# A Mamba block with linear attention and an fp8 FFN: the norms' reciprocal roots and the FFN's middle casts on ScalarE

## The chip, the core and the metric

The kernel runs on one core of a Trainium2 chip. A core has five engines with queues of their own, which run their instructions in the order of the queue: TensorE (PE, matrix products; its weight loads are listed as PEld), VectorE (DVE), ScalarE (ACT), GpSimd (POOL) and SyncE (SP), which here only issues DMAs. They share an on-chip memory (SBUF); products land in PSUM banks. The metric is the device time of one execution in microseconds (us).

## The reference

The input `x` is 8 images of 96 channels and 64 x 64 pixels; each image is a sequence of 4096 tokens. Layer 0 adds a Mamba block to `x`, layer 1 a linear attention and a two-layer FFN, each behind a norm. Cut to what is computed:

```
# layer 0:  x = x + mamba(groupnorm(x))
xz = u @ in_proj.T;  xm, z = halves of 192 channels
xm = silu(causal conv of 4 taps over xm)
dt, Bm, Cm = split(xm @ x_proj.T)                  # 6, 16, 16
delta = softplus(dt @ dt_proj.T + b)
h_t = exp(delta * A) * h_{t-1} + delta * Bm * xm   # 192 channels x 16 states
y = sum over states(h * Cm) + xm * D
out = layernorm((y * silu(z)) @ out_proj.T) * gamma + beta

# layer 1, on tokens t
t = t + (q @ (k.T @ v) * 16**-0.5, 6 heads) @ Wff + bff     # of layernorm(t)
h = relu(q16(q16(q8(layernorm(t)) @ q8(W1).T) + q8(b1)))
t = t + q16(q16(q8(h) @ q8(W2).T) + q8(b2))
```

`q8` rounds to a float of 5 exponent and 2 mantissa bits, `q16` to one of 5 and 10. A layernorm is (v - m) / sqrt(var + eps).

## The kernel before

The 8 images are 4 pairs (`p`), each sequence 8 chunks (`c`) of 512 tokens: 32 chunks in order. A chunk is 24 units (`u`, lines 711 to 765): three blocks of 64 channels (`j`), four groups of states (`g`), two halves of a group (`b`). A unit holds 128 partitions (4 states by 32 channels) by two images by 512 tokens. For unit u:

- GpSimd multiplies `dbu = du * b` three units ahead (`products_b`, L659).
- ScalarE makes `da = exp(A * delta)` into PSUM, one unit ahead, in two halves (`decay`, L681). There are two `da` buffers, so a half can start only when the scan that reads the same buffer a unit before is done.
- VectorE scans `hs = da * hs + dbu`, twice (L741), and multiplies by C from PSUM, `pr = hs * cc` (L763). In the units of `POOLED = (4, 5, 12, 13, 20, 21)` GpSimd makes this product instead, as `pooled`, at the start of the next unit (L770); those units have no product on VectorE.
- TensorE makes `cc` (`rows_c`, L671) and, for each pair of units, sums `pr` over states into the bank `y` (`sums`, L695, four matmuls). `gate` (L709) multiplies the sum by silu(z). For pooled pairs `sums` is called three units later, under `u - 3 in POOLED and u % 2 == 0`. For the last pair this would be u = 24, which does not come: its product is made, and not summed.
- ScalarE copies the last state of each unit (L719).

Everything else runs as generators, stepped by hand between the scans. `STEPS` names for each unit which chains take a step before the scans (left of the bar) and behind them (right of it); a star starts a chain. G is the group norm of the next pair; P prepares a chunk two ahead (convolution, silu, softplus, delta); E does a chunk's output projection, layernorm, residual and Gram matrix; W makes attention weights; F0 and F1 do attention and FFN for the two images of a chunk 9 earlier (`LAG`). So F0 and F1 run from chunk 9 on. The order inside the loop is the order of the program (`tc.manual_schedule()`). After the last scan the remaining chains are interleaved by `run_out`, and there, as in the prologue, the framework's scheduler orders the instructions.

An F chain (`chain_f`) goes: load tokens; attention product on TensorE (L962); residual add on VectorE (L968); layernorm of four tiles (`norm_stats` on VectorE, four GpSimd instructions, `normalise` on ScalarE, L420); transposes; cast to fp8; three hidden products (L989), each rounded to f16 (L997) and passed through bias and relu on ScalarE (L1007; on VectorE in the tail, L1003) and cast to fp8 on GpSimd (L1011); the product with W2 (L1033); rounding and bias `y16` (L1038, L1042); transposes of the residual (L1045); and the final add `res` on VectorE (L1048).

GpSimd's small work is put off: `later(kind, work)` puts it on a list, `now(kind)` issues what is there, `settle(job)` issues it early if a reader comes first. `now("norms")` stands at the start of a unit, `now("others")` behind its scans. A norm's GpSimd work is a multiplication by -1 (L412), an addition of eps (L131), a power of -1/2 (L132) and a product (L414); 128 norms run, two per E chain (8 tiles) and one per F chain (4 tiles). Silu, softplus and exp use different tables on ScalarE, so loads stand between them.

Of the kernel before, what the change touches and what calls it, by code (L numbers as in the profile page):

```python
# [39 lines left out]
    2: "| E* F0 F1 G6 F1",  # L40
    3: "F1 F0 P | F1 G6",
    4: "| E",
    5: "| W0* P F1 E",
# [22 lines left out]
def tile_mamba_linear_attention_ffn(  # L66
# [59 lines left out]
    mhalf = const.tile([128, 8], F32, name="mhalf")  # L126
    nc.vector.memset(mhalf, -0.5)

    def rsqrt(out_, var, eps):

        nc.gpsimd.tensor_scalar_add(out_, var, eps)  # L131
        nc.gpsimd.tensor_tensor(  # L132
            out_, out_, mhalf[0 : out_.shape[0], 0 : out_.shape[1]], op=ALU.pow
        )
# [264 lines left out]
    def norm_stats(src, n, tag):  # L399

        mv = p2.tile([128, n, 2], F32, tag=f"mv{tag}", name="mv")
        rstd = p2.tile([128, n], F32, tag=f"rs{tag}", name="rs")
        nmr = p2.tile([128, n], F32, tag=f"nm{tag}", name="nm")
        st = p1.tile([128, n, 6], F32, tag=f"st{tag}", name="st")
        for i in range(n):
            nc.vector.bn_stats(st[:, i, :], src[:, i, :])  # L406
        for i in range(n):
            nc.vector.bn_aggr(mv[:, i, :], st[:, i, :])


        def ends():
            nc.gpsimd.tensor_scalar_mul(nmr, mv[:, :, 0], -1.0)  # L412
            rsqrt(rstd, mv[:, :, 1], 1e-5)
            nc.gpsimd.tensor_mul(nmr, nmr, rstd)  # L414

        return rstd, nmr, later("norms", ends)

    def normalise(dst, src, norm, q):
        settle(norm[2])
        nc.scalar.activation(  # L420
            dst, src, AF.Identity, bias=norm[1][:, q : q + 1], scale=norm[0][:, q : q + 1]
        )
# [4 lines left out]
    def load_x(p, c):  # L427
# [8 lines left out]
        )  # L436
        x_next[p, c] = t

    def chain_p(p, c, s, after):
# [52 lines left out]
        nc.scalar.activation(xm, xm, AF.Silu)  # L492
        nc.scalar.activation(zs, zs, AF.Silu)
        yield
        dbl = p1.tile([C, T], F32, tag="dbl", name="dbl")
# [18 lines left out]
        for j in range(NJ):  # L514
# [5 lines left out]
            nc.scalar.activation(delta[:, j, :], ps, AF.Identity, bias=dtb[:, j : j + 1])  # L520
        nc.scalar.activation(delta, delta, AF.Softplus)
        yield
        for part in ((0,), (1, 2)):
# [17 lines left out]
    def first_p(s, after):  # L541
# [51 lines left out]
        for j in range(NJ):  # L593
# [11 lines left out]
            if not j:  # L605
                for to in ("du", "dl"):
                    s[to, 0] = p2.tile([128, 4, T], F32, tag=to, name=to)
                for b in range(2):
                    for n in range(NG):
                        for to, of, queue in (("du", "lu", nc.sync), ("dl", "ld", nc.scalar)):  # L610
# [5 lines left out]
                            )  # L616

        cs = s["cs"] = p2.tile([128, T], F32R, tag="cs", name="cs")
        nc.vector.tensor_copy(cs[64:96], ps[64:96, :])
# [91 lines left out]
    def unit(s, prev, nxt, first, u, steps):  # L711
# [16 lines left out]
        if u - 3 in POOLED and u % 2 == 0:  # L728
            sums(s, u - 3)
        if u % 2 == 0 and (u or prev is not None) and (u - 1) not in POOLED:  # L730
            sums(s if u else prev, (u or NU) - 1)
# [3 lines left out]
        if to is not None:  # L735
            products_b(to, v)
        hs = s["hs", u] = p2.tile([128, 2, T], F32, tag="hs", name="hs", bufs=3)
        dbu = s.pop(("dbu", u))
# [199 lines left out]
    def chain_f(p, c, b, banks, lane=None):  # L938
# [45 lines left out]
        h16 = []  # L984
        casts = []

# [12 lines left out]
        def relu(m):  # L999
# [6 lines left out]
            else:  # L1006
                nc.scalar.activation(h16[m], h16[m], AF.Relu, bias=b1q[:, m : m + 1])  # L1007
            casts.append(
                later(
                    "others",  # L1010
                    lambda: nc.gpsimd.tensor_copy(h8[0][:, m, :], h16[m], saturate=False),  # L1011
                )
            )

# [13 lines left out]
        yield  # L1028
        for job in casts:
            settle(job)  # L1030
        ps = psum(bank)
# [78 lines left out]

    waiting.update(norms=[], others=[])
    with tc.manual_schedule():
# [26 lines left out]
    for kind in list(waiting):  # L1139
        now(kind)  # L1140
        del waiting[kind]
    s = slots[N - 1]
    sums(s, NU - 1)
    gate(s, NJ - 1)
# [82 lines left out]
```

## Time and profile before

The median of three runs is 3163.89 us (3163.77 to 3164.42). The profiled execution spans 3160.5 us from its first to its last instruction; the rest of its time, some 3.4 us against that median, lies around the span.

| stretch, us | length | PE busy | DVE busy | ACT busy | POOL busy |
|---|---|---|---|---|---|
| prologue, 0 to 70 | 70 | 41.9 | 26.2 | 20.6 | 13.2 |
| 70 to 1000 | 930 | 733.0 | 908.0 | 630.2 | 861.1 |
| 1000 to 2000 | 1000 | 787.9 | 957.4 | 760.6 | 934.9 |
| 2000 to 3008 (last scan) | 1008 | 792.6 | 966.5 | 761.4 | 947.6 |
| tail, 3008 to 3160.5 | 152.5 | 114.3 | 77.0 | 91.0 | 83.9 |

| group | count | busy, us | mean, ns |
|---|---|---|---|
| POOL dbu, L659 | 768 | 1804.6 | 2371 |
| DVE scan, L741 (with a state pointer) | 1290 | 1573.5 | 1265 |
| ACT decay, L681 | 1474 | 1000.6 | 688 |
| POOL power, L132 | 128 | 173.3 | 1354 |
| POOL cast, L1011 | 192 | 117.6 | 622 |
| ACT table loads (L681, L492, L521) | 125 | 160.4 | 1283 |

How to read it: a line of the waits says which engine and line waited, on which engine and line, for how long in total, how often, and the longest. A line of the timeline gives start, length, engine, line, operation, output and input tiles, shape and count, and in brackets the idle time before it with what ended it. A merged line (x2, x4) covers several instructions. The first scan of chunk 15 starts at 1419.1 us; a unit with a product on VectorE takes 3.69 us, one without 2.4.

### The profile page before, as it was taken

Reading aid. Unit: us, or ns where it says so; the run is one execution under the profiler, and the core shown is the slowest. Engines: PE = TensorE matmul, PEld = TensorE weight load, DVE = VectorE, ACT = ScalarE, POOL = GpSimd, SP = SyncE. Lnnn points to the kernel's source line nnn. Section 1 sums busy time; section 2 is a strip of 40 time slices with the busy share of each in tenths; the row PEclk is TensorE's granted clock in tenths of the full one; section 3 lists DMA queues with packets and bytes.
Section 4 is the critical chain, followed back from the end, with each engine's and each line's share of the span. In section 5 each row is a group of like instructions: output and inputs, shape, how many; then the busy total and the mean of one; then the engine's idle time right before and its main releaser. Section 6 shows DMA issues by size and latency. Waiting matters only on the chain. (4 is left out here: it accounts for less than half of the span.)

```text
span 3160.5 us, 35127 instructions
## 1 busy us (share of the span) xinstructions
PE 2469.6 (78%) x9450; PEld 928.7 (29%) x9450; DVE 2935.2 (93%) x4265; ACT 2263.9 (72%) x4360; POOL 2840.7 (90%) x1921
## 2 busy tenths in 40 slices
PE   6787787878787777777777778777888778887777
PEld 2122222222222223222233323222323222332344
DVE  4999999999999999999999999999999999999945
ACT  3666666667677777777777777777877777777656
POOL 2999999999999999999999999999999999999955
PEclk8677777787778888888888877898888888877668
DMA  6655556665555667555667555567565466755322
GB/s 149 152 122 137 134 156 152 160 150 135 141 143 135 138 162 175 146 129 125 141 164 170 141 146 125 137 157 170 146 148 127 124 144 162 169 132 134 95 70 73
DMA packets 253037, 443.75 MB, mean 140 GB/s; under 512 B 37605, under 2 KB 45990, under 8 KB 252838
## 3 DMA queue, kind: packets, MB, share of 16 engines
q1 hardware_dynamic: 247846, 439.40, 56.9%
q10 hardware_dynamic: 4992, 2.11, 0.3%
q8 instruction: 74, 1.21, 0.2%
q14 instruction: 125, 1.02, 0.1%
HBM read 349.11 MB, written 92.27 MB: 140 GB/s over the span
## 5 line engine op out<-in xcount | busy, mean ns | idle before, releaser
L659 POOL TENSOR_TENSOR dbu<-du,b 128x1024 f32<-128x1024 f32 x768 | 1804.6, 2371 | 112.6 <-DVE hs L741 65.5
L741 DVE TENSOR_TENSOR_SCAN hs<-da,state,dbu 128x512 f32<-128x512 f32 x1290 | 1573.5, 1265 | 25.6 <-ACT da L681 24.6
L681 ACT ACTIVATE da<-dl,aneg 128x512 f32<-128x512 f32 x1474 | 1000.6, 688 | 665.4 <-DVE hs L741 644.2
L763 DVE TENSOR_TENSOR pr<-hs,cc 128x1024 f32<-128x1024 f32 x576 | 698.7, 1213 | 35.1 <-DVE hs L741 0.5
L695 PE MATMUL y<-pr,ssum 128*32 128x512 f32 x2816 | 585.1, 831 | 113.3 <-DVE pr L763 113.3
L770 POOL TENSOR_TENSOR pr<-hs,c 128x1024 f32<-128x1024 f32 x192 | 453.8, 2363 | 36.6 <-DVE hs L741 30.4
L459 PE MATMUL mp<-u,wk 96*64 96x512 f32 x1488 | 398.1, 658 | 66.6 <-ACT xm L477 66.4
L671 PE MATMUL cc<-cs,sel 64*128 64x512 f32 x576 | 330.0, 583 | 144.8 <-DVE pr L763 144.4
L671 PEld LDWEIGHTS cc<-cs,sel 64*128 64x128 f32 x576 | 121.6, 215 | 557.3 <-DVE pr L763 296.8
L741 DVE TENSOR_TENSOR_SCAN hs<-da,dbu 128x512 f32<-128x512 f32 x184 | 213.2, 1205 | 17.4 <-POOL dbu L659 9.9
L516 PE MATMUL mp<-dbl,dtT 12*128 12x512 f32 x186 | 158.9, 947 | 56.8 <-ACT cs L506 38.5
L695 PEld LDWEIGHTS y<-pr,ssum 128*32 128x32 f32 x2816 | 87.9, 132 | 380.6 <-DVE pr L763 201.6
L791 PE MATMUL mE<-woT,zs 128*128 128x192 f32 x744 | 146.6, 350 | 66.7 <-ACT t1e L799 45.1
L459 PEld LDWEIGHTS mp<-u,wk 96*64 96x64 f32 x1488 | 97.0, 145 | 293.6 <-issue 156.6
L132 POOL TENSOR_TENSOR rs<-rs,mhalf 128x8 f32<-128x8 f32 (+1 forms) x128 | 173.3, 1354 | 10.7
L791 PEld LDWEIGHTS mE<-woT,zs 128*128 128x128 f32 x744 | 127.3, 200 | 126.8 <-ACT t1e L799 70.5
L703 PE MATMUL y<-xm,dd 128*128 128x512 f32 x192 | 129.2, 760 | 22.4 <-DVE zs L709 21.9
L467 PE MATMUL mp<-u,wz 96*64 96x512 f32 x372 | 137.0, 825 | 4.3 <-ACT xm L485 4.3
L1011 POOL CAST h<-h 128x512 fp8e5<-128x512 f16 x192 | 117.6, 622 | 24.8 <-DVE h L1003 15.8
L719 ACT COPY state<-hs 128x2 f32<-128x2 f32 x736 | 130.1, 181 | 0.2
L420 ACT ACTIVATE o<-x,nm,rs 128x96 f32<-128x96 f32 x256 | 98.6, 455 | 36.4 <-POOL nm L414 34.4
L531 POOL TENSOR_TENSOR du<-delta,xm 128x512 f32<-128x512 f32 x93 | 117.1, 1273 | 0.0
(306 smaller groups left out, 3234.1 us busy)
## 6 DMA issues: line engine op xcount, KB each, us to landing
du<-lu SPq DMA_DIRECT2D x380, 256.0 KB, 5.5
dl<-ld SPq DMA_DIRECT2D x380, 256.0 KB, 7.9
b<-bd SPq DMA_DIRECT2D x512, 128.0 KB, 5.0
lu<-du SPq DMA_DIRECT2D x96, 256.0 KB, 5.7
ld<-delta SPq DMA_DIRECT2D x93, 256.0 KB, 2.4
c<-bd SPq DMA_DIRECT2D x128, 128.0 KB, 4.4
xg<-in_x_dram SPq DMA_DIRECT2D x32, 384.0 KB, 3.8
xr<-in_x_dram SPq DMA_DIRECT2D x32, 384.0 KB, 8.7
```

The costliest lines, as they stand in the source:

```text
L132: nc.gpsimd.tensor_tensor(out_, out_, mhalf[0 : out_.shape[0], 0 : out_.shape[1]], op=ALU.pow)
L459: nc.tensor.matmul(ps[64 * b : 64 * b + 64, :], lhsT=wk[:, k, 64 * j : 64 * j + 64], rhs=u[:, b, k : k + T], start=(k == 0), stop=(k == 3),)
L467: nc.tensor.matmul(ps[64 * b : 64 * b + 64, :], lhsT=wz[:, 64 * j : 64 * j + 64], rhs=u[:, b, 3 : T + 3], start=True, stop=True,)
L516: nc.tensor.matmul(ps, lhsT=dtT[:, j, :], rhs=dbl[0 : 2 * RANK, :], start=True, stop=True)
L659: nc.gpsimd.tensor_mul(dbu, s["du", j][:, 2 * b : 2 * b + 2, :], s["b", g][:, b, :].unsqueeze(1).to_broadcast([128, 2, T]),)
L671: nc.tensor.matmul(cc, lhsT=sel[64:128, g, b], rhs=s["cs"][64:128, :], start=True, stop=True)
L681: nc.scalar.activation(da, s["dl", j][:, 2 * b + h, :], AF.Exp, scale=aneg[:, 2 * j + h, g : g + 1])
L695: nc.tensor.matmul(s["y"][q : q + 32, :], lhsT=ssum, rhs=pr[:, h, :], start=False, stop=(g == NG - 1),)
L741: nc.vector.tensor_tensor_scan(hs[:, h, :], s.pop(("da", u, h)), dbu[:, h, :], 0.0 if first else state["last"][:, u, h : h + 1], ALU.mult, ...
L763: nc.vector.tensor_mul(pr, hs, s.pop(("cc", u)).unsqueeze(1).to_broadcast([128, 2, T]))
L770: nc.gpsimd.tensor_mul(pr, s["hs", u], s["c", g][:, b, :].unsqueeze(1).to_broadcast([128, 2, T]))
L791: nc.tensor.matmul(ps[:, 2 * k * C : 2 * (k + 1) * C], lhsT=zs[:, j, tok : tok + 128], rhs=woT[:, j].rearrange("p b c -> p (b c)"), start= ...
```

## The change

Four edits. (1) A norm's root is computed on ScalarE, as exp(-0.5 * ln(var + eps)), and ScalarE makes its negative; one product by the mean stays on GpSimd, on a new list `shifts`, issued behind `products_b`. A call `exp_and_ln` loads the table set that holds both functions behind each silu, each softplus and the prologue. (2) The casts of the FFN's middle layer go to ScalarE, directly behind the relu, in the loop; in the tail they stay on GpSimd. (3) The pair of units 20 and 21 is summed, at u = 0 of the next chunk and behind the last. (4) F0's fourth step (the normalise) moves from the front of unit 3 to the back of unit 4.

```diff
-    3: "F1 F0 P | F1 G6",
-    4: "| E",
+    3: "F1 P | F1 G6",
+    4: "| F0 E",
...
+    eps5 = const.tile([128, 1], F32, name="eps5")
+    nc.vector.memset(eps5, 1e-5)
...
-        def ends():
-            nc.gpsimd.tensor_scalar_mul(nmr, mv[:, :, 0], -1.0)
-            rsqrt(rstd, mv[:, :, 1], 1e-5)
-            nc.gpsimd.tensor_mul(nmr, nmr, rstd)
-
-        return rstd, nmr, later("norms", ends)
+        def power():
+            nc.scalar.activation(rstd, mv[:, :, 1], AF.Ln, bias=eps5)
+            nc.scalar.activation(rstd, rstd, AF.Exp, scale=-0.5)
+            nc.scalar.mul(nmr, rstd, -1.0)
+
+        def shift():
+            nc.gpsimd.tensor_mul(nmr, nmr, mv[:, :, 0])
+
+        return rstd, nmr, (later("norms", power), later("shifts", shift))
...
+    def exp_and_ln():
+        nc.scalar.preload_act_table_set("natural_log_exp_and_others")
...
         nc.scalar.activation(xm, xm, AF.Silu)
         nc.scalar.activation(zs, zs, AF.Silu)
+        exp_and_ln()
...
         nc.scalar.activation(delta, delta, AF.Softplus)
+        exp_and_ln()
...
+        if u == 0 and prev is not None:
+            sums(prev, NU - 3)
...
         now("norms")
         steps(u, 0)
         to, v = at(u + AHEAD)
         if to is not None:
             products_b(to, v)
+        now("shifts")
...
-            casts.append(
-                later(
-                    "others",
-                    lambda: nc.gpsimd.tensor_copy(h8[0][:, m, :], h16[m], saturate=False),
-                )
-            )
+            if after:
+                nc.gpsimd.tensor_copy(h8[0][:, m, :], h16[m], saturate=False)
+            else:
+                nc.scalar.activation(h8[0][:, m, :], h16[m], AF.Copy, saturate=False)
...
-        for job in casts:
-            settle(job)
...
+    sums(s, NU - 3)
     sums(s, NU - 1)
```

## The prediction

> **What bounds the kernel now.** First the page, for the busy shares.
>
> ```profile
> span 3160.5 us, 35127 instructions
> PE 2469.6 (78%) x9450; PEld 928.7 (29%) x9450; DVE 2935.2 (93%) x4265; ACT 2263.9 (72%) x4360; POOL 2840.7 (90%) x1921
> ```
>
> VectorE and GpSimd are both near full, so the waits must say which of them the other serves. I asked for VectorE's waits between 70 and 3008 us (first to last scan), then for ScalarE's and TensorE's.
>
> ```profile
> DVE hs L741 <- ACT da L681: 31.7, 43, 1.2
> DVE res L1048 <- ACT da L681: 19.8, 18, 1.7
> DVE hs L741 <- POOL dbu L659: 9.9, 1, 9.9
> DVE x L968 <- PE mE L962: 6.4, 12, 0.9
> ```
> ```profile
> ACT y L1038 <- PE mF L1033: 46.2, 23, 3.0
> ACT o L420 <- POOL nm L414: 22.4, 22, 1.1
> ```
> ```profile
> PE mF L1033 <- POOL h L1011: 40.8, 61, 1.2
> ```
>
> A scan waited for GpSimd's product once in 1536 scans, at the start. In chunks 9 to 30 VectorE is idle about 3.7 us of some 94 per chunk, and 1.4 of that are gaps of 0.1 us between a scan and the product that needs it. So VectorE's own list is the bound; freeing GpSimd pays only through the chain cast, TensorE, ScalarE, VectorE that these lines trace. The timeline of chunk 15 shows that chain in units 15 and 16 (GpSimd, TensorE, ScalarE, VectorE):
>
> ```profile
> 1478.85 0.61 POOL L1011 CAST h<-h 128x512 fp8e5<-128x512 f16 x1
> 1479.42 0.93 POOL L818 TENSOR_TENSOR t1e<-t1e,gamma 128x384 f32<-128x384 f32 x1
> 1480.29 0.61 POOL L1011 CAST h<-h 128x512 fp8e5<-128x512 f16 x1
> ```
> ```profile
> 1480.95 0.58 PE L1033 MATMUL mF<-h,w2T 128*96 128x512 fp8e5 x1 [0.85 <-POOL h L1011]
> 1481.47 2.07 PE L516 MATMUL mp<-dbl,dtT 12*128 12x512 f32 x2
> 1483.47 1.09 PE L1045 MATMUL mF<-ident,x 128*96 128x128 f32 x4
> ```
> ```profile
> 1476.32 0.73 ACT L1007 ACTIVATE h<-h,b1q 128x512 f16<-128x512 f16 x1
> 1481.58 0.58 ACT L1038 CAST y<-mF 96x512 f16<-96x512 f32 x1 [2.25 <-PE mF L1033]
> ```
> ```profile
> 1485.01 0.69 DVE L1048 TENSOR_TENSOR res<-mF,y 96x512 f32<-96x512 f32 x1 [1.04 <-ACT delta L520]
> ```
>
> The last relu ends at 1477.05, its cast at 1480.90: it stood behind GpSimd's other work. TensorE is stuck in its queue until then, then runs L516 and L1045 back to back, and VectorE stands 1.04 us. The profile names ACT for that wait, but TensorE's L1045 ends 0.45 us before `res`; I read it as the releaser.
>
> **The change, part by part.** VectorE's and SyncE's orders in the built programs are the same until the tail, apart from one memset: every microsecond won or lost in the loop is VectorE idle time. The two-chain work (F0, F1) runs from chunk 9; units 4 to 16 have it in 22 chunks (10 to 31).
>
> *Casts leave GpSimd (gain).* 138 casts of 0.615 us (85 us of GpSimd time, hidden: no one in the loop waits for GpSimd but this chain). With the cast right behind the relu, L1033 can end about 2 us sooner in unit 15, L1045 ends about 1.3 us sooner, and `res` needs 1.04. So the idle before `res` goes: 19.8 + 2.1 + 1.3 (three rows of that wait) = 23.2 us. L962, next in the same unbroken TensorE run, goes with it: 6.4. Gain 29.6 us, bounds 0 and 29.6; I take all, since the margin is 1 us. Late next would be the third delta product.
>
> *Casts land on ScalarE (loss).* No row shows the cast there. Issue to issue, the relu on the same tile takes 0.62 us (1470.19 to 1470.81), the rounding copy out of PSUM 0.48; the cast is a plain copy like the second, of the first's tile and behind it: I take 0.55. In units 2, 15 and 23 it falls where ScalarE has slack (the decay waits for the scan; over 1.3 us in unit 15). Unit 13 has none:
>
> ```profile
> 1470.81 1.29 ACT L681 ACTIVATE da<-dl,aneg 128x512 f32<-128x512 f32 x2
> 1474.43 1.30 ACT L681 ACTIVATE da<-dl,aneg 128x512 f32<-128x512 f32 x2
> ```
> ```profile
> 1471.59 2.46 DVE L741 TENSOR_TENSOR_SCAN hs<-da,state,dbu 128x512 f32<-128x512 f32 x2 [0.67 <-ACT da L681]
> 1475.54 2.45 DVE L741 TENSOR_TENSOR_SCAN hs<-da,state,dbu 128x512 f32<-128x512 f32 x2
> ```
>
> Two casts are added there, one ahead of each of these decays. The first delays the scan at 1471.59 by its whole 0.55. The second: the decay ends at 1475.12 and its scan starts at 1475.54, 0.32 beyond the usual 0.10, so 1.10 - 0.55 - 0.32 = 0.23 more. 0.78 x 22 = 17.2 us; with 0.48 it is 0.64 x 22 = 14, with 0.62 it is 0.92 x 22 = 20.
>
> *F0's normalise moves from unit 3 to unit 4 (loss).* In unit 3 it waited 1.01 us for GpSimd's root. In unit 4, which has no product on VectorE (cadence 2.4 us, not 3.7), it stands ahead of the copy L799:
>
> ```profile
> 1438.69 0.47 ACT L799 COPY t1e<-mE 128x384 f32<-128x384 f32 x1
> 1439.06 0.19 ACT L719 COPY state<-hs 128x2 f32<-128x2 f32 x1
> 1439.23 0.69 ACT L681 ACTIVATE da<-dl,aneg 128x512 f32<-128x512 f32 x1
> ```
>
> Four normalises take 1.45 from start to next start (1432.92 to 1434.37). L799 then starts at 1440.14, the decay at 1440.60, ending 1441.29; its scan began at 1440.87. Loss 0.47 x 22 = 10.3 us. Bounds: 0 (if ScalarE is early by then) and 0.6.
>
> *Norms.* GpSimd loses three instructions of 0.25, 0.24 and 1.35 us per norm, 128 norms, 236 us, hidden as above. ScalarE gets three small ones, not shown before: between the state copy (2 elements, 0.181) and a normalise (96 elements, two pointers, 0.453); I take 0.25, as 4 or 8 elements are near the copy, so 0.75 per norm. They fall in units 3, 7, 17 and 18. Unit 3 loses the 1.45 and the 1.01 of waiting and gains 1.10 (two casts) + 0.75; unit 7 has ScalarE waiting for the scan (the decay has 1.6 us of slack); in 17 the slack is 2.3 or more; in 18 the decay is then late by about 0.55 of 1.69. Cost 0; at 0.453 each (1.36) still 0. The one multiplication left on GpSimd waits for ScalarE, but stands behind dbu, and the next dbu needs a scan that ends later.
>
> *Table loads.* 128 in both built programs, of 1.283 us. They move ahead of two state copies that never waited there: 0.
>
> *Sums.* TensorE gets 4 matmuls (8 records, 1.66 us) per chunk in unit 0, where it then idles 1.5 us for ScalarE's xm: 0. If that cover is gone, `gate` in unit 1 still has over 2 us.
>
> *Start and tail.* In the prologue the two small group matmuls (25.69 and 27.21 us) now stand behind two more pairs of transposes: +2 (0 to 3), on the path to the first scan. After the last scan (152 us, ScalarE busy 91, GpSimd 84) some 20 norms become about 0.7 us shorter (1.95 on GpSimd from first start to last end, against 0.75 + 0.2 + 0.3 of handing over) but cost ScalarE 0.75 each: bounds -14 and +15, I take -1.
>
> Sum: -29.6 + 17.2 + 10.3 + 2 - 1 = -1.1 us. The profiled execution spans 3160.5, 3.4 under the median of 3163.9, so 3162.8, or 3163.
>
> A rule against the change: under "Rules for kernel authors", the Trainium skill's page "ScalarE: Activation LUTs" would have simple elementwise work on VectorE rather than ScalarE. VectorE's nearest row (the f16 relu of the tail, 0.353 us) would put 138 x 0.353 = 49 us onto the engine that bounds this kernel, and the sum would be 3163 - 17 + 49 = 3195; the row decides for ScalarE here. The same page prices a plain ACTIVATE at 186 ns plus 0.833 per element, which makes the cast 0.61 us long by estimate, 0.52 issue to issue with its overlap of 0.09; the sum by it is some 1 us lower.
>
> **Rivals.**
> - *The idle before `res` stays* (slower). ScalarE reaches unit 15 already 1.1 us late, adds a third cast, and has decays and a delta copy ahead of y16. For: ScalarE has no slack from unit 10 to 14. Against: it now stands 2.25 us there. It decides if y16's copy starts less than about 1 us sooner. Price 23: 3186.
> - *The tail gets slower.* Its queues are interlocked, and ScalarE is busy 13.3 of 15 us near 3140. Up to +15: 3178.
> - *The losses are hidden* (faster). If the casts or the moved normalise find ScalarE early, 17 + 10 do not arise, or only half: 3136 to 3150. Against: the 0.10 us between decay and scan in nearly every chunk's unit 13 and 14.
> - *The tail gains* the whole 14: 3150.
> - *GpSimd's relief speeds VectorE itself.* Scans in the trace with GpSimd busy all along take 1.260 us in the median, with it idle 1.255: worth nothing.
>
> **How the numbers follow.** Offset within 0.2% (6.3 us, about what a measurement of this kernel can tell from no change): 0.38. `res` idle stays, or the cast is dearer than 0.62: 0.21; slow tail: 0.11; losses hidden: 0.20; tail gain: 0.10. So faster 0.30, same 0.38, slower 0.32. The range of the likeliest is 3157 to 3170. For 8 in 10 it reaches to half the hidden losses and the tail's gain together (3140) and past the first rival (3190).
>
> **What would show it.** Right: no idle before L1048 in unit 16 and no wait of L1033 for GpSimd in the loop; new waits of scans for decays in units 6, 14 and 15 of 0.5, 1.0 and 0.2 us; GpSimd at about 80%, ScalarE at 77%; no more than 128 table loads. Wrong: if units 7, 17 or 18 show waits for decays, the small norms cost more than I think; if the loop keeps its length and the end does not, it was the tail.

## The result and the profile after

The changed kernel takes 3205.8 us in the median (3202.9 to 3209.3), the kernel before 3163.9 on the same chip: a ratio of 1.0134, with a 95% interval of 1.0119 to 1.0148. The prediction said 3163, in a range of 3140 to 3190. The change costs 42 us, and the time is outside the range.

The page of the changed kernel, the busy shares:

```profile
span 3205.4 us, 35922 instructions
PE 2544.6 (79%) x9706; PEld 975.9 (30%) x9706; DVE 2948.8 (92%) x4266; ACT 2414.3 (75%) x4882; POOL 2533.9 (79%) x1399
```

GpSimd fell from 90% to 79% and ScalarE rose from 72% to 75% (forecast: about 80% and 77%). VectorE, whose list of work was to stay the same, is 13.6 us busier than before. Its waits, from first scan to last (which engine waited, for whom, us in total, times, longest):

```profile
DVE hs L756 <- ACT da L693: 59.3, 81, 1.7
DVE st L408 <- ACT t1e L814: 29.1, 27, 1.3
DVE hs L756 <- POOL dbu L671: 11.3, 2, 10.0
DVE res L1058 <- ACT da L693: 9.3, 9, 1.2
DVE x L983 <- PE mE L977: 6.1, 19, 0.4
```
```profile
POOL nm L419 <- ACT nm L416: 138.7, 51, 5.2
```

Scans wait 28 us more for their decays, much as predicted. The idle before `res` only halved (19.8 to 9.3). The second line is new and was not foreseen: the norm's statistics wait for the copy of `t1e`. GpSimd's wait before the one multiplication it kept, 139 us, does no harm to VectorE, as predicted: scans wait for GpSimd hardly more than before (11.3 us against 9.9).

The two traces can be laid side by side unit by unit, since VectorE does the same work in each unit: the time from a unit's first scan to the next unit's first scan, after minus before, summed over the chunks (us; units 5, 6, 13, 14, 16 and 17 over chunks 10 to 31, where F0 and F1 both run):

| place | predicted | measured |
|---|---|---|
| start, up to the first scan | +2 | +1.9 |
| units 16 and 17 (`res`, L968) | -29.6 | -12.6 |
| units 13 and 14 (two casts on ScalarE) | +17.2 | +22.2 |
| unit 5 (decay of unit 6 late) | +10.3 | +10.9 |
| unit 6 (statistics wait for `t1e`) | 0 | +26.7 |
| units 3 and 7 (small VectorE operations get long), all chunks | 0 | +9.9 |
| all other places of the loop | 0 | +3.4 |
| tail, after the last scan | -1 | -17.4 |
| sum | -1.1 | +45.0 |

The profiled executions differ by 44.9 us. Of the 3.4 us of other places, 4.0 arise at unit 6 in chunks 1 to 9 (the rest sums to a little under zero): there the copy is not late, and TensorE's same group of matmuls ran at another clock than before. Three lines carry the error: unit 6, the small operations, and the half of the `res` idle that stayed. A fourth, the tail, is an error to the other side. The experiments take these up.

**Unit 6 in the trace.** Chunk 15, ScalarE of the changed kernel, then TensorE and VectorE (start, duration, instruction, and the idle before it with its releaser):

```profile
1461.58 0.69 ACT L693 ACTIVATE da<-dl,aneg 128x512 f32<-128x512 f32 x1 [0.49 <-DVE hs L756]
1462.21 1.53 ACT L426 ACTIVATE o<-x,nm,rs 128x96 f32<-128x96 f32 x4
1463.64 0.46 ACT L814 COPY t1e<-mE 128x384 f32<-128x384 f32 x1
1464.00 0.19 ACT L731 COPY state<-hs 128x2 f32<-128x2 f32 x1
1464.10 1.30 ACT L693 ACTIVATE da<-dl,aneg 128x512 f32<-128x512 f32 x2
```
```profile
1464.15 4.21 PE L806 MATMUL mE<-woT,zs 128*128 128x192 f32 x12 [3.34 <-ACT t1e L814]
```
```profile
1467.26 0.39 DVE L408 BATCH_NORM_STATS2 st<-t1e 128x6 f32<-128x96 f32 x2
1468.91 1.06 DVE L408 BATCH_NORM_STATS2 st<-t1e 128x6 f32<-128x96 f32 x6 [1.26 <-ACT t1e L814]
```

F0's four normalises stand ahead of the copy L814. The prediction followed the copy's other neighbour on ScalarE, the decay of unit 6, and got its 0.5 us right. It did not ask who waits for the copy itself. The copy frees bank mE (a bank is one of the pieces of PSUM that products land in); TensorE waits for it with the second half of the projection (L806). In the kernel before the same group reads:

```profile
1439.21 2.22 PE L791 MATMUL mE<-woT,zs 128*128 128x192 f32 x12 [1.35 <-ACT t1e L799]
```

So TensorE's idle grew from 1.35 to 3.34 us, and the group itself from 2.22 to 4.21 us. The granted clock, from the table of stretches (stretch, its length, busy us and instructions of PE, PEld, DVE, ACT, POOL, then the clock), shows what goes with the longer group; the first line is of the kernel before, the second of the changed one:

```profile
1439.20:1441.40 2.20, 2.19 (x13) 1.96 (x13) 2.20 (x3) 1.72 (x4) 2.20 (x2) 1.00 0.00 0
```
```profile
1464.20:1468.30 4.10, 4.10 (x13) 3.66 (x13) 3.04 (x5) 1.80 (x3) 4.10 (x2) 0.50 0.66 160
```

The same matmuls ran at full clock before and at half after. Counted from the first scan of unit 5, the copy came 1.4 us later than before and the group ended 3.4 us later; the second copy of `t1e`, which used to be ready early, held up the statistics by 1.26 us.

**The small operations in the trace.** Group norm chain G, chunk 14, unit 7, VectorE and GpSimd of the changed kernel:

```profile
1374.94 0.16 DVE L178 TENSOR_TENSOR gndev<-gnm,gnmean 96x2 f32<-96x2 f32 x1
1375.13 2.21 DVE L179 TENSOR_TENSOR gndev<-gndev 96x2 f32<-96x2 f32 x1
1377.38 0.16 DVE L180 TENSOR_TENSOR gndev<-gndev,gnmv 96x2 f32<-96x2 f32 x1
```
```profile
1374.98 2.34 POOL L671 TENSOR_TENSOR dbu<-du,b 128x1024 f32<-128x1024 f32 x1 [0.68 <-DVE gnmean L177]
```

A square of two elements takes 2.21 us, and ends within 0.02 us of the end of GpSimd's product. Before, the same operations took 0.16 us each, beside GpSimd's power operation of the norm, which the change has taken away:

```profile
1355.33 0.16 DVE L177 TENSOR_TENSOR gndev<-gndev 96x2 f32<-96x2 f32 x1
1355.52 0.16 DVE L178 TENSOR_TENSOR gndev<-gndev,gnmv 96x2 f32<-96x2 f32 x1
```
```profile
1354.59 1.67 POOL L132 TENSOR_TENSOR rs<-rs,mhalf 128x8 f32<-128x8 f32 x1
```

### The profile page after: what moved, and what is told of

Its sections match the earlier page's. It is cut to its first block, busy times and chain, and to the rows that moved or that the text cites. A ratio compares the mean times of both kernels' runs of the same rounds, so it can differ in the third digit from the quotient of the medians.

```text
span 3205.4 us, 35922 instructions
## 1 busy us (share of the span) xinstructions
PE 2544.6 (79%) x9706; PEld 975.9 (30%) x9706; DVE 2948.8 (92%) x4266; ACT 2414.3 (75%) x4882; POOL 2533.9 (79%) x1399
## 3 DMA queue, kind: packets, MB, share of 16 engines
q8 instruction: 77, 1.26, 0.2%
## 4 chain that ended last, share of the span: by engine, by line
DVE 46%; PE 21%; ACT 18%; issue 11%; POOL 2%; DVEq 0%; DMA 0%; POOLq 0%; ACTq 0%
DVE hs L756 35%; DVE pr L778 6%; ACT da L693 4%; PE y L707 4%; PE mE L806 3%; PE mp L526 3%; DVE st L408 2%; PE cc L683 2%; ACT o L426 1%; PE mp L508 1%; ACT L446 1%; PE mp L468 1%; PE mE L822 1%; PE mF L1043 1%; DVE mv L410 1%
## 5 line engine op out<-in xcount | busy, mean ns | idle before, releaser
L707 PE MATMUL y<-pr,ssum 128*32 128x512 f32 x3072 | 620.0, 804 | 114.9 <-DVE pr L778 112.6
L468 PE MATMUL mp<-u,wk 96*64 96x512 f32 x1488 | 388.7, 623 | 46.3 <-ACT xm L486 44.2
L806 PE MATMUL mE<-woT,zs 128*128 128x192 f32 x744 | 188.7, 420 | 119.5 <-ACT t1e L814 94.3
L707 PEld LDWEIGHTS y<-pr,ssum 128*32 128x32 f32 x3072 | 96.8, 129 | 405.9 <-DVE pr L778 212.8
L806 PEld LDWEIGHTS mE<-woT,zs 128*128 128x128 f32 x744 | 165.5, 249 | 176.7 <-ACT t1e L814 124.0
L526 PE MATMUL mp<-dbl,dtT 12*128 12x512 f32 x186 | 166.3, 988 | 64.4 <-ACT cs L516 49.8
L419 POOL TENSOR_TENSOR nm<-nm,mv 128x8 f32<-128x8 f32 (+1 forms) x128 | 27.4, 214 | 163.4 <-ACT nm L416 152.3
L476 PE MATMUL mp<-u,wz 96*64 96x512 f32 x372 | 145.7, 872 | 4.2 <-ACT xm L494 4.2
L508 PE MATMUL mp<-xm,xpT 128*96 128x512 f32 x186 | 114.3, 763 | 2.9 <-DVE hs L756 2.9
```

What stands on the lines that cost most here:

```text
L468: nc.tensor.matmul(ps[64 * b : 64 * b + 64, :], lhsT=wk[:, k, 64 * j : 64 * j + 64], rhs=u[:, b, k : k + T], start=(k == 0), stop=(k == 3),)
L476: nc.tensor.matmul(ps[64 * b : 64 * b + 64, :], lhsT=wz[:, 64 * j : 64 * j + 64], rhs=u[:, b, 3 : T + 3], start=True, stop=True,)
L508: nc.tensor.matmul(ps[0:C, :], lhsT=xpT[:, j, :], rhs=xm[:, j, :], start=(j == 0), stop=(j == NJ - 1),)
L526: nc.tensor.matmul(ps, lhsT=dtT[:, j, :], rhs=dbl[0 : 2 * RANK, :], start=True, stop=True)
L707: nc.tensor.matmul(s["y"][q : q + 32, :], lhsT=ssum, rhs=pr[:, h, :], start=False, stop=(g == NG - 1),)
L806: nc.tensor.matmul(ps[:, 2 * k * C : 2 * (k + 1) * C], lhsT=zs[:, j, tok : tok + 128], rhs=woT[:, j].rearrange("p b c -> p (b c)"), start= ...
```

## Experiments

The runs were made on several chips. The figure behind each time is its ratio to the kernel before on the same chip, with a 95% interval; the differences by unit are worked out from one trace of each run, against the trace of the kernel before.

### What unit 6 is made of

`swap_e_f0`: the copy first, the normalises behind it.

```diff
-    4: "| F0 E",
+    4: "| E F0",
```

> The changed kernel with the two steps of unit 4 exchanged: the copy t1e out of bank mE first, F0's normalise behind it. Theory (bank and clock): the mean loss of 1.21 us at unit 6 (22 chunks, some 26 us) comes from that copy standing behind four normalises; TensorE then waits 3.3 us for the bank, its project matmuls run at half the granted clock (one every 335 ns instead of 172), and the second t1e copy is late for bn_stats. So the copy is back at its old place, the idle ahead of the project matmuls back to about 1.4 us, their pitch to 172 ns, the wait of bn_stats in unit 6 is gone, and the loss of 0.5 us at unit 5 (decay of unit 6 behind the normalises) stays: 3206 - 26 = 3180, between 3174 and 3186. Rival (ScalarE is simply too full in units 4 to 6, the order in it does not matter): 3203 to 3209.

Measured: 3180.6 us, 1.0051 [1.0033, 1.0068] of the kernel before. The sum of the differences at unit 6 falls from 26.7 to 0.2 us, the one at unit 5 stays (11.0). TensorE's idle ahead of L806 is 1.9 us (forecast 1.4), and its clock did not come back everywhere: in 12 of 21 chunks the pitch (the time from one matmul of the group to the next; 172 ns at full clock) is still 217 to 325 ns. In chunk 15, ScalarE and TensorE:

```profile
1455.33 0.47 ACT L814 COPY t1e<-mE 128x384 f32<-128x384 f32 x1
1455.70 1.54 ACT L426 ACTIVATE o<-x,nm,rs 128x96 f32<-128x96 f32 x4
```
```profile
1455.86 3.72 PE L806 MATMUL mE<-woT,zs 128*128 128x192 f32 x12 [1.91 <-ACT t1e L814]
```

The slow group costs nothing here (0.01 us at unit 6 in each of these chunks), since it starts early. So the order of two steps is worth 25 us, and lateness alone or a slow clock alone need not cost: the next run separates them.

`fill_gap`: ScalarE's order as in the changed kernel, and TensorE given something to do in the gap.

```diff
+        if u == 4:
+            warm = ps_all.tile([128, T], F32, tag="cc", name="cc", bufs=2)
+            for _ in range(6):
+                nc.tensor.matmul(
+                    warm, lhsT=sel[64:128, 0, 0], rhs=s["cs"][64:128, :], start=True, stop=True
+                )
         steps(u, 1)
```

> The changed kernel with six matmuls added in every chunk, 128x512 into a bank of tag cc that nobody reads then, in TensorE's queue ahead of the project matmuls of unit 5; ScalarE's order, with the normalises ahead of the copy, is untouched. Theory (clock): TensorE's idle ahead of project falls from 3.3 us to about 0.8, the project matmuls come every 172 ns although their bank is freed as late as in the changed kernel, the second t1e copy is ready some 2 us sooner and bn_stats of unit 6 waits no more: 3206 - 24 = 3182, between 3177 and 3188, with 192 matmuls more. Rival (lateness of the bank alone, the clock is a bystander): the loss at unit 6 stays above 0.9 us, 3202 to 3210. Third way (the added matmuls push project back): above 3210.

Measured: 3199.7 us, 1.0106 [1.0087, 1.0125]: 6 us less, not 24, and the interval overlaps that of the changed kernel. In the traces the sum at unit 6 falls from 26.7 to 13.3 us. The six matmuls left an idle of 1.74 us, and they kept the clock in only 9 of 21 chunks. Those chunks decide the question. Chunk 13, and chunk 15, in the same run, TensorE and VectorE:

```profile
1264.17 2.22 PE L812 MATMUL mE<-woT,zs 128*128 128x192 f32 x12 [1.74 <-ACT t1e L820]
```
```profile
1267.28 1.35 DVE L408 BATCH_NORM_STATS2 st<-t1e 128x6 f32<-128x96 f32 x8
```
```profile
1461.12 3.90 PE L812 MATMUL mE<-woT,zs 128*128 128x192 f32 x12 [1.74 <-ACT t1e L820]
```
```profile
1465.56 1.06 DVE L408 BATCH_NORM_STATS2 st<-t1e 128x6 f32<-128x96 f32 x6 [0.95 <-ACT t1e L820]
```

The bank is freed equally late in both. In the 9 chunks at full clock (pitch 172 ns) unit 6 lost 0.01 us; in the 12 others (pitch 299 to 335) 0.77 to 1.37. In chunks 10 to 31 the loss needs both the late copy and the half clock. (In chunks 1 to 9 VectorE has no `res` in unit 5 and comes sooner: there the changed kernel lost up to 1.1 us at half clock without a late copy.) Why the filling held the clock in some chunks only is taken up in the last section. Elsewhere the run is worse: the gain at units 16 and 17 shrank from 12.6 to 1.1 us, which the section on the casts takes up.

`steps_before`: F0's normalise where it was, in unit 3.

```diff
-    3: "F1 P | F1 G6",
-    4: "| F0 E",
+    3: "F1 F0 P | F1 G6",
+    4: "| E",
```

> The changed kernel with the steps of units 3 and 4 as they were before: F0's normalise in unit 3, ahead of the decays of unit 4, not in unit 4. Theory: both losses of the move go (1.21 us at unit 6, 0.50 at unit 5, in 22 chunks 37 us), 0.12 at unit 4 comes, as in the run with the norm alone (3): 3206 - 34 = 3172, between 3166 and 3177. Rival (with two casts and the norm's small operations in unit 3 as well, ScalarE's decays for units 4 and 5 come late): 3180 to 3200.

Measured: 3193.8 us, 1.0086 [1.0071, 1.0101]. Units 5 and 6 are back to 0.6 us in the sum, but unit 3 now loses 17.9: the rival's mechanism. Two casts, three small operations and four normalises fill ScalarE there, and the scans of unit 4 wait 0.8 us for their decays (chunk 15). So taking the step out of unit 3 saves a loss of its own, which the prediction had not priced; putting it ahead of `E` cost twice as much.

### The casts

`casts_on_gpsimd`: the changed kernel with the casts back on GpSimd.

```diff
-            if after:
-                nc.gpsimd.tensor_copy(h8[0][:, m, :], h16[m], saturate=False)
-            else:
-                nc.scalar.activation(h8[0][:, m, :], h16[m], AF.Copy, saturate=False)
+            casts.append(later("others",
+                lambda: nc.gpsimd.tensor_copy(h8[0][:, m, :], h16[m], saturate=False)))
...
+        for job in casts:
+            settle(job)
```

> The changed kernel with the fp8 casts back on GpSimd, put off behind the scans as before; norms, sums and steps as changed. Theory (from the unit lengths of the two traces): the losses of units 13 and 14, 0.62 + 0.40 us in 22 chunks (22 us), go, and the 0.60 us that unit 16 had won comes back (13 us): 3206 - 9 = 3197, between 3190 and 3203. Rival (the sum of the prediction: casts win 29.6 and lose 17.2): 3206 + 12 = 3218.

`casts_alone`: the kernel before with nothing but the casts moved, the mirror image.

```diff
-            casts.append(later("others",
-                lambda: nc.gpsimd.tensor_copy(h8[0][:, m, :], h16[m], saturate=False)))
+            if after:
+                nc.gpsimd.tensor_copy(h8[0][:, m, :], h16[m], saturate=False)
+            else:
+                nc.scalar.activation(h8[0][:, m, :], h16[m], AF.Copy, saturate=False)
```

> The kernel before with the casts alone moved to ScalarE, behind each relu; norms, steps and sums as before (the last pooled pair of a chunk is left out of the sums, as there). Theory: per chunk units 13 and 14 lose 0.93 us, unit 16 wins 0.55, and unit 3, where ScalarE also has F0's normalise, loses up to 0.65 (as in the run with the steps of before): 22 times 1.03 is 23 us, 3187, between 3178 and 3195. Rival 1 (the prediction's own terms, -29.6 + 17.2): 3152. Rival 2 (unit 3 has room as long as the norm's small operations are on GpSimd): 3173, between 3168 and 3178.

Measured: 3199.9 us, 1.0112 [1.0092, 1.0132], and 3168.2 us, 1.0006 [0.9994, 1.0017]. In both directions the same sums appear. Casts on ScalarE cost 20.3 us at units 13 and 14 and win 12.3 at units 16 and 17 in `casts_alone`; taken off it, units 13 and 14 fall to 1.8 and the win is gone. So the casts alone do not pay, where the prediction had them 12 us ahead. `casts_alone` came out 19 us better than my expectation, mostly because unit 3 has room as long as the norm's small operations are not there (rival 2): its loss at unit 3 is 3.3 us, all of it in chunks 14 and 22, where the group norm's copy `gnm` got long.

What remains of the idle before `res` (10.8 us over 21 chunks in the changed kernel) has two sizes. With the first pair of matmuls `mp<-dbl,dtT` of unit 14 at full clock (0.53 us from one to the next) the mean idle is 0.05 us, in 11 chunks; with it at half (1.01 us), in 10 chunks, it is 1.03. TensorE of the changed kernel in chunk 12, one of the latter:

```profile
1205.24 2.07 PE L526 MATMUL mp<-dbl,dtT 12*128 12x512 f32 x2 [3.10 <-ACT cs L516]
1207.24 0.79 PE L683 MATMUL cc<-cs,sel 64*128 64x512 f32 x1
1207.97 2.02 PE L822 MATMUL mE<-idb,xr 97*128 97x96 f32 x8
1209.92 2.07 PE L526 MATMUL mp<-dbl,dtT 12*128 12x512 f32 x2
1211.92 0.79 PE L683 MATMUL cc<-cs,sel 64*128 64x512 f32 x1
1212.64 0.66 PE L1043 MATMUL mF<-h,w2T 128*96 128x512 fp8e5 x1
```

From there to L1043 TensorE has no gap. In chunk 15, with L526 at 1.12 us instead of 2.07, the same chain is nearly a microsecond ahead. The last cast of chunk 15 (ScalarE) ended 1.4 us before TensorE came to the product with W2:

```profile
1503.79 0.63 ACT L1025 ACTIVATE h<-h 128x512 fp8e5<-128x512 f16 x1
```
```profile
1505.83 1.51 PE L1043 MATMUL mF<-h,w2T 128*96 128x512 fp8e5 x3
```

So the wait for the cast was real, and behind it stood TensorE's own queue. Counted from the first scan of unit 14, the first pair starts at 1.68 us and the last cast ends at 6.78 in all 10 slow chunks and in 8 of the 11 others; what lies ahead of the pair is the same, and the clock differs. `fill_gap`, whose edit lies in unit 4, moved this clock without meaning to: the pair ran at half clock in 17 of 21 chunks, with 1.0 us of idle in the mean, and at full clock in 4, with 0.05; the idle sums to 17.3 us instead of 10.8, and these 6.5 us are more than half of the gain that units 16 and 17 lost in that run.

### The norm alone, and the sums

`norms_alone`: casts, steps and sums as before; the norm as in the change (Ln, Exp and a multiplication on ScalarE, the table loads with them).

```diff
-            nc.gpsimd.tensor_scalar_mul(nmr, mv[:, :, 0], -1.0)
-            rsqrt(rstd, mv[:, :, 1], 1e-5)
+            nc.scalar.activation(rstd, mv[:, :, 1], AF.Ln, bias=eps5)
+            nc.scalar.activation(rstd, rstd, AF.Exp, scale=-0.5)
+            nc.scalar.mul(nmr, rstd, -1.0)
...
```

> The kernel before with the norm alone changed (Ln, Exp and a multiplication on ScalarE, the last multiplication on GpSimd, table loads moved as in the change); casts on GpSimd, F0's normalise in unit 3, and, as in the kernel before, the last pooled pair of a chunk is left out of the sums. Theory: the tail's gain of 17 us belongs to the norms; the loop loses at most the 10 us of small VectorE operations that fell beside GpSimd's products: 3147 to 3157. Rival 1 (the tail was won by the casts): 3162 to 3175. Rival 2 (three small ScalarE operations a norm make decays late in units 3, 7, 17 or 18): above 3164, with new waits of scans for decays there.

Measured: 3165.6 us, 0.9998 [0.9989, 1.0008], in the range of rival 1 but not for its reason. The tail is 20.7 us shorter than before, so its gain belongs to the norms (with the casts alone it is 4.1). In the tail the median time from a norm's last aggregate on VectorE to the next normalise on ScalarE, which need not be of the same norm, fell from 2.1 to 0.8 us (worked out from the records of both traces, four aggregates to a norm). But the loop grew by 21 us, 12 of them at units 3 and 7 from the group norm's operations, where the theory allowed 10 in all.

`swap_no_sums`: the run `swap_e_f0` without the added sums.

```diff
-        if u == 0 and prev is not None:
-            sums(prev, NU - 3)
...
-    sums(s, NU - 3)
     sums(s, NU - 1)
```

> The run with the two steps of unit 4 exchanged (3180.6), without the sums of the last pooled pair of a chunk (as in the kernel before, that pair is missing from the output). Theory (TensorE has room in unit 0): 53 us less of TensorE's busy time and the same time, 3177 to 3184. Rival (the sums hold up the chain that ends in VectorE, or turn the clock's phase for unit 5 and 6): 3165 to 3174, with chunks 1 to 8 shorter by up to 1 us each.

Measured: 3187.7 us, 1.0063 [1.0048, 1.0078], 7 us more than with them on another chip; the two intervals overlap, so the times show no difference. In the changed kernel the sums cost nothing, as predicted: unit 1, where `gate` follows them, is as long as before. They are not free everywhere: in the other nine runs that have them unit 1 loses 0.8 to 4.3 us in the sum, 0.8 to 1.6 in each of one to three of the chunks 1 to 8 (3.5 us in `swap_e_f0`); in the three runs without them, this one among them, nothing. That much of the rival is so; it is made up for at other places (unit 4 loses 3.1 us here, where `swap_e_f0` wins 0.5), and why those change was not settled.

### The small operations

`g_from_psum`, on top of `swap_e_f0`:

```diff
-        nc.vector.tensor_copy(m0, mv[:, :, 0])
+        m0 = mv[:, :, 0]
...
-        nc.vector.tensor_sub(dev, m0, mean)
-        nc.vector.tensor_mul(dev, dev, dev)
-        nc.vector.tensor_add(dev, dev, mv[:, :, 1])
+        off = ps[0:C, 8:10]
+        nc.vector.scalar_tensor_tensor(off, ps[0:C, 0:2], -1.0 / 3.0, m0, ALU.mult, ALU.add)
+        nc.vector.scalar_tensor_tensor(dev, ps[0:C, 0:2], -1.0 / 3.0, m0, ALU.mult, ALU.add)
+        nc.vector.tensor_mul(off, off, dev)
+        nc.vector.tensor_add(dev, off, mv[:, :, 1])
```

> The run with the two steps of unit 4 exchanged (3180.6), and in the group norm's chain G (chunks 6, 14 and 22) no VectorE operation that reads two tiles of SBUF, and no copy from SBUF to SBUF: the copy m0 is dropped (TensorE reads the means where they are), the deviation is made twice from the bank of PSUM (once back into it), the square and the sum take one operand from there each. Theory (lock): in the changed kernel such operations of 2 elements took 1.99 to 2.24 us instead of 0.16 to 0.30, ending with the GpSimd product beside them; three in unit 3 (1.7 each over their usual time) and three in unit 7 (2.1 each) make 11 us, which go: 3169, between 3166 and 3173, and none of these operations is longer than 0.4 us. Rival (they are long for a reason of their own, or what they delay is late anyway): 3178 to 3184.

Measured: 3169.7 us, 1.0010 [1.0000, 1.0020]; 11 us won, as expected. At units 3 and 7 the sum falls by 13.5 us. The operations now take 0.13 to 0.16 us each in all three chunks, though they run beside GpSimd's products of 2.4 us. The square and the sum are the same operations as before, with one operand in PSUM; the copy is gone and the deviation is another operation, so for those two the place of the operand is not the only difference.

### Putting it together

`two_casts_back`: steps of units 3 and 4 as before, F0's first two casts on GpSimd, its third and all of F1's on ScalarE, the group norm from PSUM.

```diff
-    3: "F1 P | F1 G6",
-    4: "| F0 E",
+    3: "F1 F0 P | F1 G6",
+    4: "| E",
...
+            elif b and m < 2:
+                casts.append(later("others",
+                    lambda: nc.gpsimd.tensor_copy(h8[0][:, m, :], h16[m], saturate=False)))
...
```

> The changed kernel with three edits: the steps of units 3 and 4 as before; F0's first two casts back on GpSimd behind the scans, its third and all of F1's left on ScalarE; the group norm's small operations from PSUM. Theory: the losses of units 5 and 6 (37 us, less 3 at unit 4), of units 13 and 14 (0.62 + 0.31 in 22 chunks, 20 us) and of the group norm (11) go, the gain of 0.60 at unit 16 stays, since only the last cast held up the W2 matmul, and so does the tail's 18: 3206 - 65 = 3141, between 3133 and 3150, under both kernels. Rival (the first two casts, late on GpSimd, bring the idle before res back): 3154. Rival 2 (unit 3 is too full on ScalarE): above 3160.

Measured: 3169.5 us, 1.0009 [1.0000, 1.0018]. Units 13 and 14 lose nothing, the third cast keeps most of the gain at unit 16 (8.8 us), but unit 3 loses 16.8 (rival 2).

`norm_in_unit5`: `g_from_psum` with F0's normalise at the end of unit 5.

```diff
-    4: "| E F0",
-    5: "| W0* P F1 E",
+    4: "| E",
+    5: "| W0* P F1 E F0",
```

> The run with the group norm's operations from PSUM (3169.7), with F0's normalise moved on from unit 4 to the end of unit 5, behind the decays of unit 6 and the second t1e copy. Theory: the loss of 0.50 us at unit 5 (decay of unit 6 behind four normalises, 22 chunks, 11 us) goes, because the scan of unit 6 is followed by 2.6 us of VectorE work on the norm's statistics, under which the four normalises fit: 3159, between 3154 and 3164. Rival (the transposes of F0 in unit 6 now wait for the normalises, and hold up TensorE's queue): above 3168, with new waits in units 6 to 8.

Measured: 3158.4 us, 0.9975 [0.9965, 0.9985]. The loss at unit 5 is gone (11.0 to -0.1 us), with no new one behind it: this is the first version under the kernel before.

`three_places`: that, with F0's first two casts on GpSimd as in `two_casts_back`, the second put ahead of the product `cs`.

```diff
             elif b and m < 2:
                 casts.append(later("others",
                     lambda: nc.gpsimd.tensor_copy(h8[0][:, m, :], h16[m], saturate=False)))
+                if waiting.get("others"):
+                    waiting["others"].insert(0, waiting["others"].pop())
...
```

> The kernel of the run with F0's normalise in unit 5, and F0's first two casts back on GpSimd, the second of them put ahead of the product cs in GpSimd's queue; F0's third cast and all of F1's stay on ScalarE. Theory: the losses at units 13 and 14 (0.93 us in 22 chunks, 20 us) go, and the idle before res in unit 16 goes wholly (a further 0.4 in 22 chunks, 9 us), as the W2 matmuls then wait for no cast: 3159 - 29 = 3130, between 3122 and 3141, under the kernel before by 1%. Rival (TensorE stands before res for other reasons than the casts): 3139 to 3150. Rival 2 (the casts cannot be split without losing all of unit 16): above 3150.

Measured: 3133.6 us, 0.9902 [0.9887, 0.9917], 33 us under the kernel before on that chip and 72 under the changed one. Units 13 and 14 lose nothing. The gain at unit 16 stayed at 12.3 us instead of growing: the idle before `res` is still 11.0 us though the casts now end well ahead of the W2 matmuls. That part of the theory fell: here too it was not the casts that held up TensorE, and the clock was left as the suspect.

`fill_unit13`: 18 small fp8 matmuls into unused columns of bank mE, in TensorE's idle ahead of the first `mp<-dbl,dtT`, on top of `three_places`.

```diff
+        if u == 13 and "spare" in kept:
+            for _ in range(18):
+                nc.tensor.matmul(
+                    kept["spare"], lhsT=w1T[:, 0:128], rhs=w1T[:, 0 : T - NK * C],
+                    start=True, stop=True,
+                )
```

> The kernel of three places (3133.6), with 18 matmuls of 128x128 in fp8 added to every chunk, into columns of bank mE that nobody reads, ahead of the first of the matmuls mp<-dbl,dtT in unit 14, where TensorE stands 2.4 us. In the runs so far the idle before res in unit 16 has two values: where that first matmul pair runs at full clock (one every 0.53 us) 0.05 to 0.2 us, where it runs at half (1.01 us) about 1.0 to 1.3; in the changed kernel 11 and 10 of 21 chunks. Theory (the rest of the idle is TensorE's clock): the pair runs at full clock in nearly all chunks, the idle before res falls from 11.0 us to 2 to 5 in the sum, and the time by some 7, to 3127, between 3123 and 3131. Rival (the chunks with a slow pair are late for another reason, the clock follows): the idle stays at 9 to 13 us and the time at 3131 to 3136. Third way (the added matmuls hold up the pair, or turn the clock against a later stage): above 3136.

Measured: 3137.8 us, 0.9912 [0.9898, 0.9927], no better than without. The pair ran at full clock in 15 of 21 chunks, as many as without, so the filling did not move the clock, and the idle before `res` stayed at 9.5 us. The link held once more (full clock 0.15 us of idle in the mean, slower 1.1 to 1.3); the remedy did not. No run turned the clock there on purpose. That it is the cause of most of this last idle rests on the link, on TensorE's unbroken queue, and on `fill_gap`, where it changed and the idle with it; in `three_places` and here a few chunks at full clock still show 0.5 to 0.7 us, which is not traced further.

## Why the prediction was wrong, step by step

*What bounds the kernel*: right. VectorE's own list is the bound, each loss and gain in the loop but one is a VectorE idle, and the new ones end with ScalarE or TensorE. The one is the small operations, 9.9 us of busy time. "No one in the loop waits for GpSimd but this chain" held for waits; it left out that GpSimd can hold VectorE up with no wait being recorded.

*Casts leave GpSimd, -29.6*: the wait named was real, the size was taken at its upper bound. "With the cast right behind the relu, L1033 can end about 2 us sooner" failed, and not for the cast: counted from the first scan of unit 14, the last cast of chunk 15 ended at 6.8 us instead of 9.3, but TensorE, without a gap since L526, reached its product with W2 (now L1043) at 8.2 and ended it at 9.7 instead of 9.9, and at 10.6 in the chunks with the first L526 pair at half clock. Measured -12.6, with L968 winning nothing. The first rival had the outcome, priced at the whole 23, of which about half came; its reason, a late ScalarE, was not the one.

*Casts land on ScalarE, +17.2*: the mechanism is right; +22.2 is above the 20 that it had with the dearest cast. The cast takes 0.63 us and its successor starts 0.53 after it (taken: 0.55). Unit 13 lost 0.62 per chunk (0.55), unit 14 0.40 (0.23). ScalarE in unit 13 of chunk 15:

```profile
1496.33 0.63 ACT L1025 ACTIVATE h<-h 128x512 fp8e5<-128x512 f16 x1
1496.86 1.28 ACT L693 ACTIVATE da<-dl,aneg 128x512 f32<-128x512 f32 x2
```

*F0's normalise moves, +10.3*: this is the step that failed. The loss that it named came at its size (10.9 at unit 5), but it was less than a third of what the move cost. I moved a copy by 1.45 us and followed only the instruction behind it on its own engine. What waited for it on another engine, TensorE for the bank, was worth 26.7 us at unit 6, which the prediction put at nothing: TensorE's group started late, ran at half clock, and held up VectorE's statistics. The prediction named the copy ("it stands ahead of the copy L799"), and the one that waits for it stands in the list of TensorE's waits of the kernel before, one line away from the line that the prediction took from it:

```profile
PE mE L791 <- ACT t1e L799: 45.1, 28, 2.5
```

After the change it reads:

```profile
PE mE L806 <- ACT t1e L814: 94.3, 31, 3.9
```

*Norms*: the three small operations take 0.30, 0.21 and 0.21 us where I took 0.25 each, and hide in units 7, 17 and 18 as said, but for 1.1 us at unit 18 ahead of chunk 10. "In unit 3 ... loses 1.45 ... and gains" was right only because F0 had left it; with F0 in unit 3 it loses 17.9.

*GpSimd's relief "worth nothing"*: wrong by 10 us to the bad side. I compared the scans, whose decay lies in PSUM, with GpSimd busy and idle (1.260 and 1.255 us) and took that for all of VectorE. The small operations with both operands in SBUF are another kind. The trace of before held one such case: the copy `gnm` in chunk 6 took 2.00 us instead of 0.30, beside a product. The Trainium skill's page "SBUF — State Buffer", under "Who interferes with whom", has it that VectorE operations with two SBUF inputs, or in its two-port modes, share an exclusive port pair with GpSimd, and whichever comes second waits until the first is through. The traces here agree for GpSimd's products: 0.16 to 2.21 us and 0.30 to 1.99 us, ending with the product, and none in units 3 and 7 once no operation there had two operands, or a copy both its ends, in SBUF. For the power operation they do not: in the kernel before the same operations took 0.16 us each inside its 1.67 us, though it too has both inputs in SBUF. No run here tested why.

*Table loads and sums*: 128 loads at 1.283 us, as said; sums 0. *Start*: +1.9 for +2, a hit that is worth little: in the six other runs with this prologue the same figure lies between +0.5 and +3.6. *Tail*: -17.4 for -1, beyond the bound of -14. The chain of a norm got shorter by some 1.3 us in the median, not by the 0.7 that I took, which had only GpSimd's four instructions in it and nothing of what stood around them in its queue; that queue was not traced further. ScalarE is 11 us busier in the tail (102.4 us against 91.0), and the tail got shorter all the same.

The terms with their right size sum to what was measured, so nothing large is left unplaced; the 10 us by which the loop of `norms_alone` grew beyond the group norm's operations are not traced further.

## What to carry to other kernels

When a step is moved within an in-order queue, list for every instruction it passes who follows it on the engine and who, on other engines, reads what it writes or refills what it frees, and follow the second list to the bound engine. A gain read off one wait is an upper bound until the next thing in that queue has been found. Taking work off an engine also takes away what it kept out of the way: here a harmless operation left GpSimd and the products moved into its place.

## What the runs showed of the hardware

**TensorE's clock mostly follows how busy a stretch of 3.41 us was, not the length of one gap.** All changes of the granted clock in a trace fall on a grid of 3.413 us, to within 0.01 us. Counting the busy share of TensorE in each such stretch of the loop, from the matmul records (kernel before, and changed kernel):

| at full clock, stretch busy | fell to half next, before | after |
|---|---|---|
| under 0.45 | 49 of 50 | 65 of 69 |
| 0.45 to 0.65 | 49 of 128 | 44 of 83 |
| over 0.65 | 21 of 350 | 19 of 379 |

At half clock it rose only after a stretch at least 85% busy (all of 120 rises before, 128 of 129 after). Only about half of such stretches were followed by a rise. So an idle of 1.9 us is enough where it falls whole into one stretch of the grid, and the same gap in another chunk does nothing. In `swap_e_f0` the 12 chunks that fell are those whose gap ahead of L806, 1.9 us or more, lies whole in one stretch (busy 0.28 to 0.44); in 8 of the 9 others the grid cuts it, with 0.9 to 1.6 us in the longer part. In `fill_gap` the longer part is 0.9 to 1.4 us in the 9 chunks that kept the clock and 1.1 to 1.7 in the 12 that did not. That the same holds for `fill_unit13` is likely and was not worked out. The Trainium skill's page "TensorE: Matmul & The Clock Gate", Part 1, has a free-running window of 3413 ns, and agrees in that; it has the clock fall after an idle window of about 3.4 us, and there the measurement differs: here a window a little over half idle was enough.

**A VectorE operation of two elements can take 2.2 us** if both inputs lie in SBUF and GpSimd runs a product; in the profile it shows as a long duration, not as a wait, so that the list of waits is silent and only VectorE's busy time (13.6 us up for the same instructions, 9.8 of them in these operations) gives it away.
